# V loads asked for one window step earlier, first columns turned on GpSimd, and a different order at three joints of a fused attention, convolution and MLP kernel

## The chip, the cores and the metric

The kernel runs on one core of a Trainium2 chip. The metric is the device time of one execution in microseconds; the number given for a kernel is the median of its runs. Engines are called by their names: TensorE (PE, with its weight loads PEld), VectorE (DVE), ScalarE (ACT), GpSimd (POOL) and SyncE (SP), which issues the DMAs.

## The reference

The input x is 2 x 56 x 56 x 384 in float32. Two layers follow each other, everything in float32.

- Layer 0: `x = x + neighborhood_attention(layer_norm(x))`, with 12 heads of 32 channels. Each pixel attends to the 7 x 7 pixels around it (shifted inwards at the borders), with a relative position bias. Then `x = x + gelu(layer_norm(x) @ w1 + b1) @ w2 + b2`, 384 to 1536 and back.
- Layer 1: `p = layer_norm(x) @ w_in + b_in` (384 to 768 channels), a depthwise 3 x 3 convolution `local` of p, four exponential scans of it (`y = 0.6 * y_before + 0.4 * local`, along the rows in both directions and along the columns in both directions), `mixed = 0.25 * (their sum) + local`, then `x = x + layer_norm(mixed) @ w_out + b_out`, and again an MLP with gelu.

## The kernel before

The kernel writes out the order of each engine's instructions by hand; nothing is rescheduled behind it. An engine works through its list in order, and each instruction waits for what it reads and for the buffer that it writes.

**Attention.** The 2 x 56 x 56 pixels are 14 groups of 8 rows (448 pixels); each group is four windows of 8 x 14 queries, so 56 windows. A window has three units, one for four heads. The loop at L691 makes one step per unit, `s` from 0 to NU + 3 with NU = 168; `k = s % 12` is the step in the group and `hg = s % 3` the unit in the window. In step s, PE makes the scores of unit s (L508) into the two halves of a PSUM tile `sc`, then the values of unit s - 2 (L544 from `pts` and `vt`, and L550, the sums of the numerators through a matmul with ones). VectorE adds the bias to each half (L521), ScalarE takes the exponential (L528), VectorE adds up the numerators of unit s - 1 (L534, L536). After the last unit of a window the output is copied (`take`, L477), the sums are transposed and the 11 columns that are needed copied by GpSimd to `history` (`gather`, L481 and L482), inverted and spread (`invert`, L486 and L488), and multiplied in (`divide`, L492 and L494). Into most steps one more piece is put: queries, keys and values of later groups (L385, L423), or the projection of a finished tile (L569), whose result VectorE adds to the residual `xr` one step later (L577). In the last two groups (from `END` on) there is nothing left to compute ahead, and projections stand only in the steps of `THEN`.

`vt`, the values of a window's keys, comes back from `v_d` in DRAM in two or three DMAs when a `Window` is made (L464). SP's list in a step is, in order: stores of finished tiles (`store_all`, L629), loads of residuals (`load_residual`, L558), loads of later groups and biases (L301, L315), one of six parts of the MLP weights in the last steps (L612), and, where a window begins, its `vt`.

Before the loop, the first group is normalized and its queries, keys and values are made. Its four tiles are measured and applied in two halves (L632 to L643); group 1 and group 2 are normalized by ScalarE (`normalize_x`, L240), and turned by PE (`channels_of`, L356).

**Passes.** After the attention two passes go over groups of two to four tiles of 128 tokens. The first makes the MLP of layer 0 (12 chunks `hidden`, L1035 and L1044, then one `tokens` per tile, L1051, with the residual in L1381) and the projection `project_in` of the group before. The second (from L1413 on) makes the MLP of layer 1, with `measure` (transposes of `mix_d` by PE and statistics, L1238) of the next group beside its hidden chunks and `project_out` (L1258) after them.

**Beside.** Convolution and scans of layer 1 lie on VectorE beside the passes. `Beside` (L113) is a planner: `go(worth)` adds `worth` times a rate to a budget, and steps of the waiting jobs are issued until their costs have used it up; `until(name)` issues everything up to a named job. `Band` jobs make the convolution and the row scans of some rows, `Columns` jobs the column scans of one of 6 channel blocks of an image. A `Columns` job first turns half the image so that columns lie along the free axis (`turn`, four copies of 128 x 392, L1176, on ScalarE); the job behind another `Columns` is turned by the one before it, so that only the first of each image turns its own lines at its start. The second pass needs the second image's mixed values from group `half_way` on: at the end of group `half_way - 2` the planner runs `until((1, NI - 1))` and the group's `mx` is loaded (L1439, L1440).

## Time and profile before

| | |
|---|---|
| median of 3 runs | 2735.04 us (2734.52 to 2737.29) |
| the profiled execution | 2735.71 us, of which the span from first to last instruction is 2733.8 us |
| mean granted TensorE clock | 0.991 |
| DMA, mean over the span | 109 GB/s, 31% of the 16 engines' time |
| attention | up to about 708 us, its last projections to 722 us |
| first pass | from about 724 us to 1716 us |
| second pass | to the end; `mx` of the second image's first group is asked for at 2155 us |

A row of the timeline gives start, duration, engine, source line, operation, output and inputs, how many instructions are merged, and in brackets how long the engine was idle before it and what ended that. A line of the list of waits gives who waited for whom, the us in total, how often, and the longest. A row of a table of windows gives for each engine the busy us and the number of instructions, then the granted clock of TensorE (1.00 is full speed), the share of the DMA engines and GB/s. Many of PE's waits are shorter than 1 us; those that the change touches are shown in the prediction.

### The profile page before, as it was taken

How to read it: one execution, taken by the hardware profiler on the slowest of the kernel's cores; microseconds unless marked ns; L12 is line 12 of the kernel's file. 1: busy time of each engine (PE TensorE's matmuls, PEld its weight loads, DVE VectorE, ACT ScalarE, POOL GpSimd, SP SyncE). 2: the span in 40 equal slices, each digit the busy share in tenths (PEclk: the TensorE clock that was granted, in tenths of full speed). 3: DMA queues.
4: the chain of work that ended last, by engine and by line, in shares of the span. 5: the costliest groups of instructions: out<-in, count | busy, mean ns of one | idle time of the engine just before them, and what ended most of it. 6: DMA issues, size and time to landing. Idle time of an engine off the chain costs nothing. (4 is left out here: it accounts for less than half of the span.)

```text
span 2733.8 us, 36207 instructions
## 1 busy us (share of the span) xinstructions
PE 2686.1 (98%) x14975; PEld 1505.5 (55%) x14975; DVE 1663.0 (61%) x2449; ACT 907.5 (33%) x1455; POOL 239.1 (9%) x256
## 2 busy tenths in 40 slices
PE   8999999999899999999999999999999999999998
PEld 4566656665655555555545555455555555555565
DVE  3778767777421188688988889888798422221110
ACT  4555555554322332222344422311233211111111
POOL 0111111110211100000000000000000011110100
PEclk9999999999999999999999999999999999999999
DMA  6322444224411122232355444433454410011000
GB/s 206 131 93 92 155 165 150 76 74 154 155 35 38 63 88 103 86 129 101 120 184 195 180 151 154 163 128 114 147 200 158 151 47 25 28 44 35 29 12 16
DMA packets 131887, 298.91 MB, mean 109 GB/s; under 512 B 10646, under 2 KB 87552, under 8 KB 129408
## 3 DMA queue, kind: packets, MB, share of 16 engines
q1 hardware_dynamic: 131712, 296.50, 31.2%
q8 instruction: 119, 1.95, 0.3%
q14 instruction: 56, 0.46, 0.1%
HBM read 180.86 MB, written 115.61 MB: 108 GB/s over the span
## 5 line engine op out<-in xcount | busy, mean ns | idle before, releaser
L1035 PE MATMUL mm<-hT,w 128*128 128x512 f32 (+2 forms) x1872 | 778.7, 571 | 3.9 <-ACT hid L1044 3.8
L1051 PE MATMUL y<-w,hid 128*128 128x384 f32 x2352 | 764.8, 486 | 0.0
L1051 PEld LDWEIGHTS y<-w,hid 128*128 128x128 f32 x2352 | 445.0, 190 | 305.2 <-issue 0.5
L1035 PEld LDWEIGHTS mm<-hT,w 128*128 128x128 f32 x1872 | 352.5, 191 | 378.1 <-issue 343.1
L1044 ACT ACTIVATE hid<-mm,chan 128x512 f32<-128x512 f32 (+2 forms) x312 | 206.0, 661 | 744.8 <-PE mm L1035 744.7
L1129 DVE SCALAR_TENSOR_TENSOR loc<-pt,taps,loc 128x990 f32<-128x990 f32 (+9 forms) x336 | 377.0, 1122 | 8.3
L521 DVE TENSOR_TENSOR pts<-sc,bias 119x448 f32<-119x448 f32 (+3 forms) x336 | 220.8, 699 | 97.9 <-PE sc L508 97.0
L528 ACT ACTIVATE pts<-pts 119x448 f32<-119x448 f32 (+3 forms) x336 | 206.5, 641 | 194.6 <-DVE pts L521 194.4
L222 POOL TENSOR_TENSOR rs<-rs,mhalf 128x4 f32<-128x4 f32 (+4 forms) x67 | 87.3, 1303 | 1794.5 <-DVE rs L219 1788.0
L385 PE MATMUL ps<-hT,wqkv 128*128 128x448 f32 x504 | 211.5, 558 | 0.6 <-ACT hT L361 0.4
L1051 PE MATMUL y<-w_out,mx 128*128 128x384 f32 x588 | 193.7, 489 | 3.2 <-DVE xc L1258 3.2
L1035 PE MATMUL mm<-hT,w_in 128*128 128x512 f32 (+2 forms) x468 | 191.7, 568 | 0.6 <-ACT hT L254 0.6
L1381 DVE TENSOR_TENSOR xc<-y,xa 128x384 f32<-128x384 f32 x49 | 27.3, 557 | 252.1 <-PE y L1051 251.7
L1432 DVE TENSOR_TENSOR xc<-y,xc 128x384 f32<-128x384 f32 x49 | 27.2, 556 | 219.5 <-PE y L1051 169.2
L1051 PEld LDWEIGHTS y<-w_out,mx 128*128 128x128 f32 x588 | 112.5, 191 | 84.7 <-issue 6.8
L508 PEld LDWEIGHTS sc<-qT,kT 32*100 32x100 f32 (+3 forms) x3168 | 97.8, 171 | 91.3 <-DVE pts L521 17.7
L240 ACT ACTIVATE xn<-xc,sh,rs 128x384 f32<-128x384 f32 x98 | 64.7, 698 | 248.6 <-DVE sh L233 248.4
L1035 PEld LDWEIGHTS mm<-hT,w_in 128*128 128x128 f32 x468 | 88.8, 190 | 101.5 <-issue 91.6
L214 DVE BATCH_NORM_STATS2 st<-xi 128x6 f32<-128x384 f32 x98 | 50.3, 554 | 154.2 <-PE xi L1238 154.1
L508 PE MATMUL sc<-qT,kT 32*100 32x112 f32 (+3 forms) x3168 | 130.9, 279 | 8.6 <-DVE pts L521 7.8
L385 PEld LDWEIGHTS ps<-hT,wqkv 128*128 128x128 f32 x504 | 90.0, 191 | 79.5 <-issue 74.8
L254 ACT ACTIVATE hT<-tp,chan 128x512 f32<-128x512 f32 (+2 forms) x117 | 79.4, 750 | 152.5 <-PE tp L251 152.4
(88 smaller groups left out, 2421.5 us busy)
## 6 DMA issues: line engine op xcount, KB each, us to landing
bias<-in_bias_t SPq DMA_DIRECT2D x16, 1344.0 KB
loc<-loc_d SPq DMA_DIRECT2D x24, 784.0 KB
mixed<-mix_d SPq DMA_DIRECT2D x24, 784.0 KB
mix_d<-mixed SPq DMA_DIRECT2D x24, 784.0 KB
xa<-x_d SPq DMA_DIRECT2D x22, 768.0 KB
p_d<-mx SPq DMA_DIRECT2D x10, 1536.0 KB
mx<-mix_d SPq DMA_DIRECT2D x10, 1536.0 KB
pt<-p_d SPq DMA_DIRECT2D x18, 560.0 KB
```

Source lines behind the costliest of these rows:

```text
L214: nc.vector.bn_stats(st[:n, i, :], x)
L222: nc.gpsimd.tensor_tensor(rs, rs, mhalf[:n, :k], ALU.pow)
L240: nc.scalar.activation(out[:, k, :], x[:, k, :], AF.Identity, bias=self.sh[:n, k : k + 1], scale=self.rs[:n, k : k + 1],)
L254: nc.scalar.activation(dst[:, c, : len(xs) * n], tp, AF.Identity, bias=col(b, c), scale=col(g, c))
L385: nc.tensor.matmul(ps, lhsT=wqkv[:, c, m * P : (m + 1) * P], rhs=hT[:, c, half_of(n)], start=c == 0, stop=c == NC - 1,)
L508: nc.tensor.matmul(sc[i // 2][: w.keys, i % 2, c * TT : (c + 1) * TT], lhsT=kT[d, hg, w.keys_at + r * w.kc : w.keys_at + (r + w.rows) * w.kc],
L521: nc.vector.tensor_tensor(self.of(half), sc[half][:n, :, : self.m * TT].rearrange("p h (c q) -> p h c q", q=TT), self.w.bias[:n, 4 * self. ...
L528: nc.scalar.activation(self.of(half), self.of(half), AF.Exp)
L1035: nc.tensor.matmul(ps[:, : n * P], lhsT=w[:, c, m * P : (m + 1) * P], rhs=hT[:, c, : n * P], start=c == 0, stop=c == NC - 1,)
L1044: nc.scalar.activation(t[:, : n * P], ps[:, : n * P], AF.Gelu, bias=col(b1, m))
L1051: nc.tensor.matmul(ps, lhsT=t[:, k * P : (k + 1) * P], rhs=w[:, m, :], start=m == 0, stop=m == len(lhs) - 1,)
L1129: nc.vector.scalar_tensor_tensor(to, pt[:, lo + dy - self.top : hi + dy - self.top, xt : xt + n], self.tap(dy, dx), to, ALU.mult, ALU.add,)
```

## The change

The change has these parts.

- **V one step ahead.** A window, and with it the DMAs of its `vt`, is made in the last step (`hg == 2`) of the window before it instead of in its own first step; `vt` has three buffers instead of two. The first window is made ahead of the loop.
- **No history.** The sums of all windows are no longer kept: `gather` copies to a small tile `totals`, and `invert` multiplies two comparisons into a running tile `good` of 128 x 11. The two comparisons over 128 x 616 at the end are gone, and the reduction reads 11 columns. `turned` and `rec_t` share one buffer, and the operand of the value bias takes a buffer of `vs`.
- **First instructions.** Both halves of the first group are measured ahead of the first `apply`; group 2 is normalized by ScalarE ahead of the keys of group 1 instead of behind them.
- **First columns.** A `Columns` job that turns its own first lines does so with GpSimd's `tensor_copy`; the other turns stay on ScalarE.
- **A step dropped.** After the last tile of the last group of the first pass there is no `beside.go(ROW)`; ROW is 6.2.
- **Second image's first group.** For the group `half_way`, `measure` stands beside the hidden chunks 5, 7, 9 and 11 instead of 3, 5, 7 and 9, and its norm is closed at chunk 11 instead of 10.

```diff
--- before.py
+++ after.py
@@ -286,7 +286,8 @@
 
 
     BLOCKS = -(-NC * TT // HD)
-    history = lp.tile([P, len(windows), BLOCKS], F32, name="history")
+    good = lp.tile([P, BLOCKS], F32, name="good")
+    nc.vector.memset(good, 1.0)
     ones_hd = lp.tile([P, HD], F32, name="ones_hd")
     nc.vector.memset(ones_hd, 1.0)
 
@@ -433,7 +434,7 @@
 
     def shift_by_values(pool, psum, wproj, shift):
 
-        bv = pool.tile([P, NC, P], F32, name="bv")
+        bv = pool.tile([P, C], F32, name="vs", bufs=2).rearrange("p (c q) -> p c q", c=NC)
         for c in range(NC):
             nc.vector.tensor_copy(bv[:, c, :], col("b_v", c).to_broadcast([P, P]))
         ps = psum.tile([P, GT], F32, name="ps", tag="pt")[:, :C]
@@ -458,7 +459,7 @@
             self.keys = self.rows * self.kc
             self.keys_at = KEYS_AT[self.j]
             self.bias = biases[self.b, pr, pc]
-            self.vt = lp.tile([P, 3, C], F32, name="vt", bufs=2)
+            self.vt = lp.tile([P, 3, C], F32, name="vt", bufs=3)
             for c, a in enumerate(self.starts):
                 r = self.b * H + self.r0 + a
                 nc.sync.dma_start(
@@ -477,18 +478,23 @@
             nc.scalar.copy(self.og, o.rearrange("p c (r w) -> p c r w", r=QR))
 
         def gather(self):
-            turned = lp.tile([P, BLOCKS, HD], F32, name="turned")
+            turned = lp.tile([P, BLOCKS, HD], F32, name="turned", tag="turned")
             nc.vector.transpose(turned.rearrange("p a b -> p (a b)"), sums[:, : BLOCKS * HD])
-            nc.gpsimd.tensor_copy(history[:, self.i, :], turned[:, :, 0])
+            self.totals = sm.tile([P, BLOCKS], F32, name="totals")
+            nc.gpsimd.tensor_copy(self.totals, turned[:, :, 0])
 
         def invert(self):
             rec = sm.tile([P, BLOCKS], F32, name="rec")
-            nc.vector.reciprocal(rec, history[:, self.i, :])
+            nc.vector.reciprocal(rec, self.totals)
+
+
+            for edge, inside in ((SUM_MAX, ALU.is_le), (1.0 / SUM_MAX, ALU.is_ge)):
+                nc.vector.scalar_tensor_tensor(good, self.totals, edge, good, inside, ALU.mult)
             self.wide = lp.tile([P, BLOCKS, HD], F32, name="wide")
             nc.gpsimd.tensor_copy(self.wide, rec.unsqueeze(2).to_broadcast([P, BLOCKS, HD]))
 
         def divide(self):
-            rec = lp.tile([P, BLOCKS * HD], F32, name="rec_t")
+            rec = lp.tile([P, BLOCKS * HD], F32, name="rec_t", tag="turned")
             nc.vector.transpose(rec, self.wide.rearrange("p a b -> p (a b)"))
             rec = rec[:, : NC * TT].rearrange("p (c r w) -> p c r w", c=NC, r=QR)
             nc.vector.tensor_tensor(self.og, self.og, rec, ALU.mult)
@@ -630,15 +636,17 @@
 
 
     tps = [any_bank() for c in range(NC)]
-    for h in range(0, NT, 2):
-        norm = Norm(sm)
+    halves = [Norm(sm) for h in range(2)]
+    for h, norm in enumerate(halves):
         for k in range(2):
-            norm.add(k, [xgs[0][:, h + k, :]])
+            norm.add(k, [xgs[0][:, 2 * h + k, :]])
         norm.close(2, TT)
+    for h, norm in enumerate(halves):
         for k in range(2):
-            norm.apply(k, xgs[0][:, h + k, :], xgs[0][:, h + k, :])
+            x = xgs[0][:, 2 * h + k, :]
+            norm.apply(k, x, x)
             for c in range(NC):
-                turn_x(0, h + k, c, tps[c])
+                turn_x(0, 2 * h + k, c, tps[c])
     for c in range(NC):
         take_x(0, c, tps[c])
     nc.vector.tensor_scalar_mul(bq, chan[:, COL["b_qk"] : COL["b_qk"] + NC], HD ** -0.5)
@@ -663,11 +671,11 @@
     for t in tiles_of(1)[:2]:
         value(t, any_bank)()
         store_all()
+    for k in range(NT):
+        normalize_x(2, k)
     for m in range(NC, 2 * NC):
         query_or_key(1, m, any_bank)()
     store_all()
-    for k in range(NT):
-        normalize_x(2, k)
     for c in range(NC):
         channels_of(2, c, any_bank)()
     load_bias(0, 3)
@@ -685,6 +693,7 @@
 
     units, ws, to_project, ahead, taking = {}, {}, [], [], []
     ng = len(groups_a)
+    ws[0] = Window(0)
 
 
     END, THEN = ng - 2, (7, 9, 11, 13, 16, 19, 22)
@@ -718,6 +727,8 @@
             ectx.close()
             wm = ctx.enter_context(tc.tile_pool(name="w_mlp", bufs=1, side="right"))
             w1, w2, w_parts = weights(0)
+        if s < NU and hg == 2 and s + 1 < NU:
+            ws[i + 1] = Window(i + 1)
         if s >= NU - UG - 4 and hg == 2 and w_parts:
             w_parts.pop(0)()
         if s == NU:
@@ -737,8 +748,6 @@
             sctx.close()
             ps_s = sctx.enter_context(tc.tile_pool(name="a_pss", bufs=4, space=PSUM))
         if s < NU:
-            if hg == 0:
-                ws[i] = Window(i)
             units[s] = Unit(ws[i], hg)
             units[s].scores()
         new, before, last = units.get(s), units.get(s - 1), units.pop(s - 2, None)
@@ -799,12 +808,7 @@
         project(t, any_bank)()
     store_all()
 
-
     bad, flag = const.tile([P, 1], F32, name="bad"), const.tile([1, 1], mybir.dt.int32, name="flag")
-    every = history.rearrange("p w k -> p (w k)")
-    good = lp.tile(every.shape, F32, name="good")
-    nc.vector.tensor_scalar(good, every, SUM_MAX, 1.0, ALU.is_le, ALU.mult)
-    nc.vector.scalar_tensor_tensor(good, every, 1.0 / SUM_MAX, good, ALU.is_ge, ALU.mult)
     nc.vector.tensor_reduce(bad, good, axis=AX.X, op=ALU.min)
     nc.vector.tensor_scalar(bad, bad, -1.0, 1.0, ALU.mult, ALU.add)
     sctx.close()
@@ -1168,12 +1172,12 @@
                     for h in range(2):
                         nc.sync.dma_start(out=flat(self.loc[h]), in_=self.rows(loc_d, h))
 
-            def turn(self):
+            def turn(self, copy):
                 c, t = len(self.lines), half("line", "work")
                 for i in range(0, HALF, QUARTER):
                     for h in range(2):
                         at = slice(c * HALF + i, c * HALF + i + QUARTER)
-                        nc.scalar.copy(
+                        copy(
                             t[:, i : i + QUARTER, h * HALF : (h + 1) * HALF],
                             self.loc[h][:, :, at].rearrange("p h w -> p w h"),
                         )
@@ -1181,7 +1185,8 @@
 
             def steps(self):
                 if not self.lines:
-                    self.turn()
+
+                    self.turn(nc.gpsimd.tensor_copy)
                     yield 2.5
                 mixed, behind = [], None
                 for c in range(2):
@@ -1189,7 +1194,7 @@
                     for i in range(0, HALF, QUARTER):
                         yield from both_ways(t[:, i : i + QUARTER], t[:, i : i + QUARTER])
                         if c == 0 and i == 0:
-                            self.turn()
+                            self.turn(nc.scalar.copy)
                             for h in range(2):
                                 mixed.append(half("mixed", "out", 3))
                                 nc.sync.dma_start(out=flat(mixed[h]), in_=self.rows(mix_d, h))
@@ -1207,7 +1212,7 @@
                     if c == 0:
                         beside.behind()
                 if isinstance(behind, Columns):
-                    behind.turn()
+                    behind.turn(nc.scalar.copy)
                 for h in range(2):
                     def store(h=h):
                         nc.sync.dma_start(out=self.rows(mix_d, h), in_=flat(mixed[h]))
@@ -1241,12 +1246,13 @@
                 parts.append(ps.rearrange("p c q -> p (c q)"))
             norm.add(k, parts)
 
-        def measure_beside(m, g, ahead):
+        def measure_beside(m, g, ahead, late=0):
 
             n = dgroups[g][1]
-            if m % 2 == 1 and 0 < m // 2 <= n:
-                measure(ahead[0], ahead[2], m // 2 - 1)
-            if m == 10:
+            k = (m - late) // 2 - 1
+            if m % 2 == 1 and 0 <= k < n:
+                measure(ahead[0], ahead[2], k)
+            if m == min(10 + late, NHID - 1):
                 ahead[2].close(n)
 
         def project_out(g, mx, x, inner):
@@ -1380,7 +1386,8 @@
                 ps = tokens(hid, w2, k)
                 nc.vector.tensor_tensor(x2[:, k, :], ps, x[:, k, :], ALU.add)
                 norm.add(k, [x2[:, k, :]])
-                beside.go(ROW)
+                if g < last or k < n - 1:
+                    beside.go(ROW)
             norm.close(n)
             waiting = g, x2, norm
             if g + 2 <= last:
@@ -1415,7 +1422,7 @@
             for m in range(NHID):
                 hid.append(hidden(w1, m, hT, n, "L1_conv_b1"))
                 if g < last:
-                    measure_beside(m, g + 1, ahead)
+                    measure_beside(m, g + 1, ahead, 2 if g + 1 == half_way else 0)
                 beside.go(MLP_D)
             res = x3
             if g < last:
```

## Prediction

> **What bounds the kernel now.** I read the page's busy times first, then the list of PE's waits, then the stretches around each wait in the timeline and in tables of windows.
>
> ```profile
> PE 2686.1 (98%) x14975; PEld 1505.5 (55%) x14975; DVE 1663.0 (61%) x2449; ACT 907.5 (33%) x1455; POOL 239.1 (9%) x256
> ```
>
> TensorE is busy for 98% of the span, and the change leaves every matmul in place. So it can win only PE's 47.7 us of idle time and the time in which PE works at a lower clock. The waits of PE:
>
> ```profile
> PE ps L356 <- DVE xg L226: 7.8, 2, 6.0
> ...
> PE o L544 <- DMA vt<-v_d: 6.1, 4, 3.1
> PE mm L1035 <- ACT hid L1044: 3.8, 1, 3.8
> PE xi L1238 <- DMA mx<-mix_d: 3.5, 1, 3.5
> PE y L1051 <- DVE xc L1258: 3.2, 1, 3.2
> PE ps L356 <- ACT xg L240: 2.4, 4, 1.6
> ```
>
> Each part of the change has its row here: the first instructions (7.8 and 2.4), V (6.1), the first columns (3.8), the first group of the second image (3.5), and the step dropped at the end of the first pass (3.2). Columns: us in total, times, longest. The clock comes on top. In windows of 5 us in the last windows of the attention (busy us of PE, PEld, DVE, ACT, POOL; then the granted clock):
>
> ```profile
> 660.00:665.00 5.00, 5.00 (x26) 2.37 (x22) 0.60 (x2) 0.33 (x1) 0.00 (x0) 0.50 0.25 88
> ...
> 685.00:690.00 5.00, 2.53 (x40) 1.70 (x40) 1.38 (x3) 0.17 (x1) 0.00 (x0) 0.62 0.81 261
> ```
>
> At 660 PE is busy throughout at clock 0.50, and VectorE stands nearly still behind it: the projection L569 takes 4.21 us there and 2.20 at 668.59. So a stall costs its own length, and then some microseconds at half speed.
>
> **The rule on the clock, against the rows.** The Trainium skill, "TensorE: Matmul & The Clock Gate", section "What's actually happening", has the clock halve after an idle window of about 3.4 us. By that rule only the stalls of 3.81 and 3.47 us would drag a slow stretch behind them, and the clock would bring about 5 us less than below. The rows show more: half speed also follows the 3.23 us stall, and begins at 658.9, with PE merely thinned out (0.26 us busy in that microsecond). I follow the rows.
>
> **Opening (to 52 us).** Both halves of the first group are now measured before either is applied. VectorE's 1.6 us of statistics for tiles 2 and 3 (6.20 to 7.83) move into the wait for the power on GpSimd and ahead of the first applies. The second applies start at 7.07 (4.59 + 1.6 + 0.87) instead of 8.64, so 1.57 us earlier. PE's weight loads take 0.33 us instead of 0.19 until 13.99, and if that point stays put half is lost again: 0.8 to 1.57, I take 1.2. Moving ScalarE's four normalizations (2.49 us) ahead of the keys removes 1.59 + 3 x 0.28 = 2.43 us, as ScalarE is free from 37.6 and PE turns that tile only at 43.8. The key copies behind them come up to 0.8 us later; their banks are wanted again after 44, so nothing. The clock is 0.80 and 0.86 in the two windows after 45: (0.20 + 0.14) x 5 = 1.7 us. Sum 5.3, bounds 3 and 6. The bias operand now waits for a stored V tile's buffer; with its store out by 36 and PE reading at 46, that is covered.
>
> **V (590 to 708 us).** Before, vt was asked for in the step that starts the window, behind that step's store and residual load in SP's queue:
>
> ```profile
> 672.23 0.43 SPq L612 DMA_DIRECT2D w<-in_L_conv_w  x1
> 672.77 0.42 SPq L629 DMA_DIRECT2D x_d<-xr  x1
> 681.78 0.33 SPq L558 DMA_DIRECT2D xr<-in_x  x1
> 682.21 1.53 SPq L464 DMA_DIRECT2D vt<-v_d  x2
> ```
>
> The residual load waits for the store to land, which is behind the bias and 768 KB of weights, and vt behind it: 10 us late. Now the same loads stand one step earlier, and ahead of that step's weights: this one at about 672. A third buffer removes the wait for the values of the window before last. So all four vt waits go. In steps: the one at 656.7 gets back 1.24, then 2.01 in its projection and 0.45 in the next scores: 3.7. The one at 682.6 gets back 4.1, of which 0.5 is lost again to VectorE, whose 3.85 us of work in that step is next late: 3.6. The last gets 0.8. The slow projection at 678.44 (2.0) follows a wait for VectorE at 675.56, not for vt, so I count half: 1.0. Sum 9.1. SP now meets V's own stores sooner, in the step after they are issued; behind it stand only stores and loads for later steps.
>
> Against it stand 112 additions to VectorE, two updates of good per window. The nearest row is a 128x4 scalar_tensor_tensor at 0.16 us (bounds 0.07, a small memset, and 0.23, the 128x11 reciprocal): 0.32 per window. Up to 590 us VectorE waits for scores after them, 97 us in all, which covers them; uncovered they would cost 18. Of the ten windows after 590 I charge a third: 1.0. The two 128x616 checks at the end (0.47 + 0.80) were not on the path: PE restarts at 723.84, before they end. Net 8.1, bounds 3 (the stalls alone less 3.2) and 12.
>
> **First columns (1395 us).**
>
> ```profile
> 1394.55 0.92 ACT L1176 COPY line<-loc 128x392 f32<-128x392 f32 x1 [5.10 <-DMA loc<-loc_d]
> ...
> 1396.48 2.54 ACT L1176 COPY line<-loc 128x392 f32<-128x392 f32 x3 [1.02 <-DMA loc<-loc_d]
> ...
> 1400.26 11.06 PE L1035 MATMUL mm<-hT,w 128*128 128x512 f32 x18 [3.81 <-ACT hid L1044]
> ```
>
> ScalarE stands in front of these copies from 1389.45, three PSUM buffers fill, and PE stops. On GpSimd the copies block nobody: the next power in its queue comes 75 us later, in the second image 50 us. Gain 3.81, and weight loads 0.86 us apart instead of 0.43 until 1406.4, so 3.0 more: 6.8, bounds 3.5 and 7.5. In the second image ScalarE waits likewise at 1971, but no PE wait hangs on it: nothing. The price of a copy on GpSimd: nearest row wide, 352 elements in 0.48, so 0.53 each, 2.1 for four (ScalarE: 3.5). The rule that speaks against it is in "SBUF — State Buffer", "SBUF: two separate sides": GpSimd and a VectorE operation with two SBUF inputs lock each other out for a whole instruction. The rows agree that it bites: the power takes 1.01 alone and 1.75 to 2.4 beside VectorE's scans. At worst each copy waits out a scan of 1.79, 9.3 us for four. Only the scans of these lines wait for that, and no matmul, so the sum stays.
>
> **Dropped step (1716 us).**
>
> ```profile
> 1711.45 2.26 DVE L1076 TENSOR_TENSOR_SCAN both<-decay,loc 128x1008 f32<-128x1008 f32 x1
> ...
> 1715.31 0.62 DVE L1258 SCALAR_TENSOR_TENSOR xc<-y,rs,xa 128x384 f32<-128x384 f32 x1
> ...
> 1715.98 6.47 PE L1051 MATMUL y<-w_out,mx 128*128 128x384 f32 x14 [3.23 <-DVE xc L1258]
> ```
>
> Without the last go(ROW), taps and a scan (1706.33 to 1713.7) no longer stand before the norm's close and L1258. The wait of 3.23 goes, and 4.2 us at half clock behind it: 2.0. Sum 5.2, bounds 3 and 5.5.
>
> **Second image's first group (2165 us): here I expect no gain.** The dropped 6.2 credits are not given back. In the built order of VectorE, what is left after the last output add L1432 of the group before grows from the four updates at 2151.34 to four updates and three scans with their end fixes: 3.22 to about 8.7 us.
>
> ```profile
> 2150.86 0.56 DVE L1432 TENSOR_TENSOR xc<-y,xc 128x384 f32<-128x384 f32 x1 [1.94 <-PE y L1051]
> 2151.34 3.22 DVE L1202 SCALAR_TENSOR_TENSOR mixed<-line,mixed 128x392 f32<-128x392 f32 x4
> ...
> 2155.02 2.93 SPq L1224 DMA_DIRECT2D mx<-mix_d  x2
> ...
> 2164.59 1.51 PE L1238 MATMUL xi<-ident,mx 128*128 128x128 f32 x6 [3.47 <-DMA mx<-mix_d]
> ```
>
> The stores, and mx behind them, come 5.5 us later. Two chunks are 2 x 2.57 = 5.14 us. New wait: 3.47 + 5.5 - 5.14 = 3.8. Change: -0.4, bounds -4 and +5.6 (wait and slow clock both gone). Closing the norm at chunk 11 leaves about 2.7 us to the scale, under 3.9 us of matmuls and a second y buffer: nothing.
>
> **Sum.** 5.3 + 8.1 + 6.8 + 5.2 - 0.4 = 25.0. I take off 1.0 because the attention's last loads now come in less time and the wait at 723.84 (2.24, behind xa's landing) may grow. 24.0 from the span of 2733.8 gives 2709.8; the profiled execution was 2735.71 and gives 2711.7; the median of the runs, 2735.04, gives 2711.
>
> **Rivals.** (a) The two chunks do what they say: PE finds mx landed, 3.5 + 2.1 more: 2705. For it: two chunks exceed the old wait. Against it: the count of VectorE's leftover work. (b) The attention's end keeps its half clock: between scores PE still waits for VectorE at each step, as at 597 us without any vt wait. Then only the waits of 6.1 less 3.2 are won there: 2716. (c) Slower: the updates of good stand on the path. They have two SBUF inputs and are issued beside GpSimd's copy of wide (0.48). If each window's scores waited for 0.32 + 0.48 us, 56 windows would cost 45: 2735 - 25 + 45 = 2755. It decides from 0.45 us per window on. Against it: after the reciprocal VectorE often waits 1.2 to 2.6 us for scores.
>
> **Chances.** My forecast 0.56, own range 2706 to 2717; (a) 0.14; (b) 0.22; (c) 0.04; between no change and (b), several parts failing together, 0.04. From these: faster by over 0.2% (5.5 us, about what a measurement can tell from no change) 0.93, within 0.03, slower 0.04. The range 2702 to 2721 takes in (a), (b) and the bounds of the parts.
>
> **What would show it.** Right: no PE wait for vt, for hid at L1035 or for L1258; one for mx of about 4 us that stays; clock 1.00 after the former 1400 and 1716; first L385 matmul near 9.5; scores from about 46.5. Wrong: mx waits gone; clocks of 0.5 at the attention's end; the updates of good followed at once by L521 with PE waiting for it.

## The result and the profile after

The changed kernel takes 2716.53 us (median of 4 runs, 2715.67 to 2720.46), the kernel before beside it 2735.57 us: ratio 0.9931, 95% interval 0.9916 to 0.9947, so 19.0 us faster. The forecast was 2711 with a range of 2702 to 2721. A second comparison on another chip gave 2719.87 against 2734.78, ratio 0.9943 (0.9930 to 0.9957), 14.9 us. The forecast gain of 24 lies above both. The profiled execution took 2715.98 us with a span of 2714.2.

The busy times of the page, and the first rows of the list of PE's waits:

```profile
PE 2673.1 (98%) x14975; PEld 1500.2 (55%) x14975; DVE 1685.2 (62%) x2560; ACT 900.2 (33%) x1447; POOL 249.7 (9%) x264
```

```profile
PE sc L514 <- DVE pts L527: 8.2, 17, 1.1
PE ps L357 <- DVE xg L226: 7.0, 1, 7.0
PE tp L251 <- DVE bad L812: 6.6, 1, 6.6
PE xi L1243 <- DMA mx<-mix_d: 4.8, 1, 4.8
PE o L550 <- DMA vt<-v_d: 3.9, 6, 1.1
```

Gone are the waits for `hid` (3.8) and for `xc` of the output projection (3.2). The opening's 7.8 and 2.4 are one wait of 7.0. Two rows speak against the forecast: V is still waited for, six times, and the wait at the entry to the first pass (L251), 2.2 before, is 6.6.

The span fell by 19.6 us, PE's busy time by 13.0, its idle time by 6.6. With every matmul still there, less busy time is half clock that went, and stalls too short to be listed (the run with four times the updates shows such stalls). The windows of the attention's end that were shown for before:

```profile
660.00:665.00 5.00, 4.34 (x74) 2.74 (x74) 3.71 (x10) 1.56 (x4) 2.04 (x4) 1.00 0.60 192
...
685.00:690.00 5.00, 4.91 (x86) 3.08 (x82) 4.15 (x8) 2.43 (x5) 0.60 (x2) 1.00 0.31 91
```

Both stand at clock 1.00 (0.50 and 0.62 before). Only the second is a sign of the change: in the three kernels without V of the experiments below the window at 660 is at 1.00 too, and the one at 685 at 0.50 to 0.53.

**Where the time went, part by part.** The same VectorE instructions (transposes of the sums, additions of projections and of `tokens`) can be found in every profile; they are called marks here. How much earlier or later each comes than in the profile before tells what lies between two of them. I did this for the changed kernel and for all the kernels of the experiments below, since single profiles turned out to scatter. In the table, "with" are the profiles of kernels that hold the part, "without" those that do not (the one of before is 0 by definition); minus is earlier, in us.

| part, by the time of before | forecast | with | without | difference of means |
|---|---|---|---|---|
| opening, to 110 | -5.3 | -2.9 to -6.7 in nine profiles, mean -4.9 | 0, 1.1, -0.4, -0.5 | -4.9 |
| attention, 110 to 594 | 0 | 0.0 in each | 0 to 0.4 | 0 |
| V, 594 to the last unit at 708 | -8.1 | -6.8, -4.9, -6.5, -7.0, -6.9 | 0, 1.6, -0.5, -1.4 | -6.3 |
| 708 to the first pass's output at 751 | +1.0 | 5.2, 6.0, 6.1, 5.9, 0.8 | 0, -0.9, -0.5, -2.2 | +5.7 |
| first columns, 1376 to 1440 | -6.8 | -7.1 to -7.2 in ten profiles | 0, -0.5, -1.2, -0.5 | -6.6 |
| dropped step, 1705 to 1801 | -5.2 | -5.1 to -5.2 in ten profiles | 0, 0, -0.1, -1.7 | -4.8 |
| second image's group, 2151 to 2213 | +0.4 | 1.7, 1.1, 1.4, 2.4, 1.5, 1.5 | 0, 1.3, 1.0, -1.3 | +1.4 |

The differences add up to 15.5 us, between the two measured gains; the forecast's column to 24.0. V's two rows scatter most: from 594 to 751 together the five profiles with the part range from 1.1 later to 6.1 earlier, the four without from 0.6 later to 3.6 earlier. (Profiles of kernels that alter a part in a third way are left out of its row.)

### The profile page after: what moved, and what is told of

Read it like the earlier page. It is cut to its first block, busy times and chain, and to the rows that moved or that the text cites. A ratio compares the mean times of both kernels' runs of the same rounds, so it can differ in the third digit from the quotient of the medians.

```text
span 2714.2 us, 36305 instructions
## 1 busy us (share of the span) xinstructions
PE 2673.1 (98%) x14975; PEld 1500.2 (55%) x14975; DVE 1685.2 (62%) x2560; ACT 900.2 (33%) x1447; POOL 249.7 (9%) x264
## 5 line engine op out<-in xcount | busy, mean ns | idle before, releaser
L386 PE MATMUL ps<-hT,wqkv 128*128 128x448 f32 x504 | 211.9, 559 | 1.4 <-ACT vs L431 0.8
L1439 DVE TENSOR_TENSOR xc<-y,xc 128x384 f32<-128x384 f32 x49 | 27.2, 555 | 218.2 <-PE y L1055 167.8
L514 PEld LDWEIGHTS sc<-qT,kT 32*100 32x100 f32 (+3 forms) x3168 | 96.9, 169 | 91.2 <-DVE pts L527 18.5
L514 PE MATMUL sc<-qT,kT 32*100 32x112 f32 (+3 forms) x3168 | 130.1, 277 | 9.1 <-DVE pts L527 8.2
L386 PEld LDWEIGHTS ps<-hT,wqkv 128*128 128x128 f32 x504 | 90.2, 191 | 80.6 <-issue 74.8
```

Of the source, the lines that this page charges most:

```text
L386: nc.tensor.matmul(ps, lhsT=wqkv[:, c, m * P : (m + 1) * P], rhs=hT[:, c, half_of(n)], start=c == 0, stop=c == NC - 1,)
L514: nc.tensor.matmul(sc[i // 2][: w.keys, i % 2, c * TT : (c + 1) * TT], lhsT=kT[d, hg, w.keys_at + r * w.kc : w.keys_at + (r + w.rows) * w.kc],
```

## Experiments

The theory after the first profile: four of the forecast's terms hold; V's gain is given back before the first pass begins, through the landing of `xa` and GpSimd's queue; the dropped step's work comes back as a later `mx`. Rivals: the parts are not independent; the updates of `good` cost; DMA bandwidth and no queue is what makes things late; the list's own name for the wait at L251, the reduction `bad`.

### The four parts alone

Each is the kernel before with some hunks of the diff: the two hunks of the first instructions; those of V and of the history; those of `turn`; those of `measure_beside` and of the dropped `go`.

> The kernel before with the two reordered joints of the opening alone. Theory from the trace of the changed kernel: 6.4 us faster, 4.7 of it by 68 us and 1.7 more at 75 to 80 us, where the clock stays at 1.00 instead of 0.66; so about 2729. Rival, the forecast's term: 5.3, so 2730. A second rival: the 1.7 of clock is not owed to the reordering and comes and goes; then 4.7, 2730.5, and the trace shows the slow stretch at 75 to 80 us again.

Measured: 2729.89 us beside 2733.11, ratio 0.9984 (0.9978 to 0.9991). 4.5 us are won by 68 us and none at 75 to 80, where this profile has a slow stretch as before; the second rival describes it. That the stretch is not owed to the reordering is seen in the changed kernel itself. Windows of 5 us in the first profile of the changed kernel, then in its second:

```profile
70.00:75.00 5.00, 5.00 (x80) 3.20 (x75) 3.87 (x11) 2.54 (x7) 0.71 (x2) 1.00 0.37 121
75.00:80.00 5.00, 5.00 (x54) 3.11 (x53) 3.07 (x6) 2.66 (x6) 0.00 (x0) 1.00 0.44 127
```

```profile
70.00:75.00 5.00, 5.00 (x40) 3.33 (x41) 3.10 (x8) 2.03 (x5) 0.71 (x2) 0.50 0.31 102
75.00:80.00 5.00, 5.00 (x51) 2.74 (x50) 2.65 (x5) 1.53 (x3) 0.00 (x0) 0.84 0.12 42
```

The same code at the same place, once at 1.00 and once at 0.50 and 0.84: (0.50 + 0.16) x 5 = 3.3 us of difference that no line of the code makes, behind the same stall (PE is busy for 3.76 and 3.77 us between 65 and 70). The Trainium skill, "TensorE: Matmul & The Clock Gate", section "What's actually happening", says that the window in which activity is judged runs freely, and that the number of slow matmuls at a kernel's start therefore varies from run to run. These rows show such a variation in the middle of a kernel; that the free window is its cause is not shown. The runs of one kernel on one chip vary as well (the 21 of this one from 2724.9 to 2732.7). So a clock term that is read from one profile, as those of the forecast were, is a draw and not a constant.

> The kernel before with V asked for one step ahead, three vt buffers and the running good instead of the history, alone. Theory from the trace: the part wins 6.8 us net up to the last unit of the attention and gives 5.2 back before the first pass begins, because the inputs of the first pass (xa) and the last residuals come only 8.8 us earlier: net 1.6 us, 2733.5. Rival, the forecast: 8.1 less 1.0, so 7.1 us, 2728.5. Rival: the updates of good on VectorE cost more than they seem, net slower than 2735.6. Without the opening's gain DMA times are not moved relative to PE, so the waits for vt should look like those of the changed kernel: about six, 4 us together.

Measured: 2734.89 us beside 2733.11, ratio 1.0004 (0.9996 to 1.0013). V and the running `good` alone bring nothing that can be measured. The forecast's 7.1 is outside the interval (at best -1.1 us). In the profile 4.9 us are won between 594 and 708 and 6.0 given back by 751; the wait at L251 is 7.3. The theory's course is right, won and then given back; its net of 1.6 us faster is not, as it lies outside the interval too. The waits for `vt` were expected to be six with 4 us, and are four with 2.8. The last rival, a net loss, is not excluded: the interval reaches to 3.6 us slower.

> The kernel before with the first columns of each image turned by GpSimd, alone. Theory: one mechanism with one place, 7.2 us as the trace shows between 1390 and 1410, so 2728.4; the forecast's term 6.8, 2728.8. Rival: part of the 7.2 is owed to the earlier parts of the change (other distances on VectorE); then 3.8 to 6.

Measured: 2728.65 us, ratio 0.9984 (0.9977 to 0.9991), 4.5 us, which is the rival's number (3.8 to 6). But its reason is not seen: the profile has 7.1 between 1376 and 1440, the same as the profiles with all parts. Part of the difference is the draw of the clock in the profile before: where this part is not changed, the same stretch of other profiles is 0.5 to 1.2 shorter. That leaves 6.6, a little above the interval, which reaches to 6.3; the rest was not found.

> The kernel before with the dropped step at the end of the first pass and the later measurement of the second image's first group, alone. Theory from the trace: 5.2 won at 1716, 1.2 lost at 2165 where the wait for mx grows from 3.5 to 4.8 us: net 4.0, 2731.6. Rival, the forecast: 5.2 plus 0.4, 2730.0. Rival: the two chunks hide the wait in this setting, 5.2 plus 5.6, 2724.8. The four parts alone should add up to 19 if they are independent.

Measured: 2728.53 us, ratio 0.9987 (0.9978 to 0.9995), 4.6 us: the theory's 4.0 fits. (The expectation misquotes the forecast: its term for the second image's group was a loss of 0.4, so 4.8 for both, which fits as well.) In the profile -5.1 at 1716 and +1.7 at 2165. The wait for `mx` is 3.8 here; in kernels without this part it was 3.4 to 4.3.

### The changed kernel beside them

> The changed kernel itself, beside the kernel before on the chip of the other runs of this group. The four parts alone came to 3.2, -1.8, 4.5 and 4.6 us by the medians, 10.5 together. If the parts are independent, this kernel is about 10 to 12 us faster here, and the 19 us of the first comparison owed something to its chip or its few runs. Rival: the parts help each other, above all the opening and V at the attention's end, and it is again 17 to 20 us faster.

Measured: 2719.87 us, 14.9 faster than before (11.8 to 19.1 by the interval), between the two expectations. The four parts alone came to 10.5, each with 2 us of uncertainty. By the marks in their own stretches the single parts win 4.6 (opening), 7.1 (columns) and 3.5 (end) and lose 1.1 (V), 14.1 together, and this profile of the changed kernel wins 14.2. So there is no sign of parts that help each other much; but both comparisons of the whole (14.9 and 19.0) lie above 10.5, and whether a few us of it come from parts together stays open.

### The entry to the first pass

The end of the attention in the changed kernel. Rows of PE, SyncE's queue and GpSimd, by the timeline:

```profile
694.62 13.81 PE L575 MATMUL ps<-wproj,og 128*128 128x384 f32 x42
...
700.95 2.23 SPq L564 DMA_DIRECT2D xr<-in_x  x5
703.22 0.95 SPq L602 DMA_DIRECT2D xa<-x_d  x2
...
709.76 0.71 POOL L222 TENSOR_TENSOR rs<-rs,mhalf 128x2 f32<-128x2 f32 x1 [5.29 <-DMA xa<-x_d]
710.44 3.85 POOL L569 TENSOR_TENSOR xr<-xr,shift 128x384 f32<-128x384 f32 x4
...
715.02 1.51 PE L251 MATMUL tp<-ident,xn 128*128 128x128 f32 x6 [6.59 <-DVE bad L812]
```

PE's last projections end at 708.4. The additions of `shift` to the last four residuals stand in GpSimd's queue behind the norm's power, which waits for `xa`; the residual additions on VectorE wait for them, and PE, as it seems, for the PSUM of the projections: it begins 0.14 us behind the end of the last residual addition (714.88), as in the kernel before (0.15, from 723.69). From the start of the power to PE's first L251 it is 5.26 us here, 5.28 before (718.56 to 723.84) and 5.27 in the second profile (714.11 to 719.38): 0.68 of power, 3.85 of additions, 0.7 behind. In the run with the old chunks below, the projections ended 4 us later (712.4) and PE began at 715.00 all the same, 5.28 behind its power. So PE begins when `xa` lets it. `xa` is asked for behind a residual load that waits until a store has landed, and that store stands behind 768 KB of weights. (In the last windows of this profile the load that waits for such a store goes out 5.1 to 9.2 us behind it; behind the two stores with no weights right ahead of them, at 645 and 652, it is 2.5 and 3.7.) In the profile before this was so too, but PE came later and waited 2.2. V's gain of 13.2 at 708 (with the opening's) met an `xa` that landed only 8.8 earlier.

First edit: `xa` ahead of the residuals (the pools are opened with it), and the additions ahead of the norm.

```diff
         store_all()
+        if s == NU:
...
+            xs = {g: load_group(x1f, groups[g], "xa") for g in range(2)}
         while load:
             load_residual(load.pop(0))
...
         take()
+    for t in list(loaded):
+        add_bias(t)
     norm = norm_of(xs[0], groups[0][1], sm)
```

> The changed kernel, with the loads of xa ahead of the last residual loads in SyncE's queue and the additions of shift to the last residuals ahead of the norm's power in GpSimd's queue. Theory: the 5.2 us that were given back at the attention's end hang on the landing of xa (707.99) and on the power of its norm, which stands in GpSimd ahead of the four additions that the last projections wait for; then PE takes up the first pass at about 709 instead of 715.0, 6 us faster than the changed kernel, and the wait of 6.6 shrinks to about 1. Rival: the reduction named in the list of waits (bad, L812) is what PE waits for, or the landing of the last residual loads; then nothing, or under 2 us.

Measured: 2714.91 us beside 2719.87 of the changed kernel and 2734.78 of before, ratio to before 0.9928 (0.9915 to 0.9942): 5.0 better than the changed kernel by the medians, but not in the way expected. The wait at L251 shrank to 3.8 only, and PE began at 713.55. Now GpSimd's five additions waited for the residuals (they run from 705.88), the statistics of `xa` stood on VectorE behind the first residual addition until 707.38, and the power in GpSimd behind the five additions until 710.65. The second half of this edit, the additions ahead of the norm, had turned GpSimd's queue around for the worse.

Second edit, added to the first: `vt` straight behind `store_all()`, ahead of the residual.

```diff
         store_all()
...
+        if s < NU and hg == 2 and s + 1 < NU:
+            ws[i + 1] = Window(i + 1)
         while load:
             load_residual(load.pop(0))
...
-        if s < NU and hg == 2 and s + 1 < NU:
-            ws[i + 1] = Window(i + 1)
```

> The same, and a window's vt is asked for right behind the stores of its step, ahead of the load of the residual. Theory: the six waits for vt (3.9 us together) stay because vt stands in SyncE's queue behind a residual load that waits until a store has landed; they go, and since the attention's end no longer gives it back, the kernel is 10 us faster than the changed one (4 more than the one above). Rival: VectorE's work per step is next late, and PE waits for pts instead: 0 to 2 us more than the one above. Second rival: DMA bandwidth is what makes vt late; then the waits for vt stay.

Measured: 2712.72 us, ratio 0.9920 (0.9906 to 0.9934), 2.2 better than the one above, which the intervals do not tell apart. No wait for `vt` is left. But the edit moved less than it was meant to. A residual is loaded in the step of its store, and in the last windows that is mostly an earlier step than the one that asks for `vt`. So a single `vt` passes a residual load (it goes out at 652.86, the residual at 655.06), and the next three still stand behind one. SyncE in this run:

```profile
665.95 0.41 SPq L635 DMA_DIRECT2D x_d<-xr  x1
675.21 0.33 SPq L564 DMA_DIRECT2D xr<-in_x  x1
675.59 1.50 SPq L465 DMA_DIRECT2D vt<-v_d  x2
```

Those three go out 1.9 to 2.4 us earlier than in the run above. So the order of the queue has a part in it, but this run does not decide between queue and bandwidth; and three profiles with the old order have only 0.2 to 0.5 us of these waits. PE's waits for `pts` and `sum` of VectorE rose from 8.7 to 10.1, and the marks at 708 were 1.9 later than in the run above, as the rival has it. (In the next run, without this edit, they are 11.3.) The gain lies behind 708, where the residual load now goes out at 699.02 instead of 702.71.

Third: the first edit without the additions, GpSimd's queue left as it is.

> The changed kernel with the loads of xa ahead of the residual loads, and GpSimd's queue left as it is (power first, then the four additions). In the run that also turned GpSimd's queue around, the additions ran from 705.88 to 710.69 and the power only at 710.65, so PE began again at 713.55. Theory: with xa early and the power first, the power is done before the last residuals land, the four additions end near 711, and PE begins again at 711 to 712: 6 to 7 us faster than the changed kernel (5.0 by the medians with both edits). Rival: the power still waits for xa, since DMA traffic and not the queue's order delays it; then PE begins again at 714 or later, and it is within 3 us of the changed kernel.

Measured: 2712.97 us beside 2736.41, ratio 0.9917 (0.9904 to 0.9931), some 5.5 better than the changed kernel (whose ratios to before were 0.9931 and 0.9943). GpSimd and PE in this run:

```profile
707.07 0.71 POOL L222 TENSOR_TENSOR rs<-rs,mhalf 128x2 f32<-128x2 f32 x1 [2.28 <-DVE rs L219]
707.75 3.87 POOL L569 TENSOR_TENSOR xr<-xr,shift 128x384 f32<-128x384 f32 x4
...
713.05 0.84 PE L251 MATMUL tp<-ident,xn 128*128 128x128 f32 x6 [0.81 <-DVE bad L813]
```

The power waits for VectorE's own work and no longer for a transfer, PE waits 0.8, and the clock stays up (0.84 us for these six transposes instead of 1.51). The list still names `bad`, which follows the last residual addition at once; in the kernel before it came at 724.95, after PE had begun. So it was never what PE waited for. Between 594 and 751 this profile gains 7.9, the ones of the changed kernel 1.6 and 0.4. (The two runs below that leave this stretch as it is gain 1.1 and 6.1 there, so a single profile proves little; the four kernels with `xa` early gain 4.6 to 7.9.) PE begins 1 to 2 us later than I had expected, since its own projections ended at 712.2 here. So one order in SyncE's queue, and not V's own path, held most of what V should have brought: 4 to 7 us, by the runs' times and by the profiles.

### The second image's first group

```diff
-                beside.go(MLP_D)
+                beside.go(MLP_D + (ROW / NHID if g == 0 else 0.0))
```

> The changed kernel, and the 6.2 credits of the dropped step are given back in the second pass, 0.52 with each of the twelve hidden chunks of its first group. Theory: the wait for mx of 4.8 us at 2165 comes from work of the beside planner that the dropped step left over; VectorE's leftover after the last output addition falls from about 8.7 to 3.2 us, mx lands 5.5 us earlier and the wait goes: 5 to 7 us faster than the changed kernel. Rival: VectorE has no room in that first group, PE waits there for the statistics, and the gain is eaten: within 2 us. Second rival: the transfer of mx itself is slow, and 2 to 4 us of the wait stay.

Measured: 2711.98 us beside 2719.87 and 2734.78, ratio to before 0.9920 (0.9906 to 0.9933): 7.9 better than the changed kernel by the medians. VectorE ahead of the stores in the changed kernel, then in this one, from the output addition L1439 on:

```profile
2130.61 0.56 DVE L1439 TENSOR_TENSOR xc<-y,xc 128x384 f32<-128x384 f32 x1 [1.17 <-PE y L1055]
2131.09 1.78 DVE L1084 TENSOR_TENSOR_SCAN line<-decay,line 128x784 f32<-128x784 f32 x1
...
2136.51 3.20 DVE L1207 SCALAR_TENSOR_TENSOR mixed<-line,mixed 128x392 f32<-128x392 f32 x4
...
2150.82 1.51 PE L1243 MATMUL xi<-ident,mx 128*128 128x128 f32 x6 [4.80 <-DMA mx<-mix_d]
```

```profile
2130.78 0.56 DVE L1439 TENSOR_TENSOR xc<-y,xc 128x384 f32<-128x384 f32 x1 [1.94 <-PE y L1055]
2131.25 3.22 DVE L1207 SCALAR_TENSOR_TENSOR mixed<-line,mixed 128x392 f32<-128x392 f32 x4
...
2146.03 0.82 PE L1243 MATMUL xi<-ident,mx 128*128 128x128 f32 x6
```

The scans are no longer behind the last addition, and PE does not wait. Between 2151 and 2213 this profile gains 5.1, where the changed kernel loses 1.1 and 1.4: 6.4 us. In the first group, where the work went, nothing is lost (the marks from 1801 to 2126 stay at -20.1).

The other side, the old chunks with the dropped step:

```diff
-                    measure_beside(m, g + 1, ahead, 2 if g + 1 == half_way else 0)
+                    measure_beside(m, g + 1, ahead)
```

> The changed kernel with the second image's first group measured beside chunks 3, 5, 7 and 9 again, the dropped step left out as in the changed kernel. The forecast's sum for the wait for mx was 3.47 + 5.5 - 5.14. By it the wait is 4.8 + 5.1 = 9.9 us here and the kernel 5 us slower than the changed one. Rival: the matmuls of the two chunks move behind the wait but the clock is at half speed behind the longer wait, 7 us or more. Second rival: mx lands no later for the dropped step, the later chunks were not needed; then the wait is near 4 and the time the same.

Measured: 2723.33 us beside 2736.41, ratio 0.9957 (0.9943 to 0.9971). Row of the waits:

```profile
PE xi L1243 <- DMA mx<-mix_d: 9.9, 1, 9.9
```

9.9 is the sum 4.8 + 5.1 to the tenth, so two chunks are worth what the forecast took for them. The ratio is 5.5 us above the mean of the changed kernel's two. The stretch from 2151 to 2213 is 6.4 us longer than in the mean of its two profiles, so some 1.3 of it would be half clock behind the longer wait (the window of 5 us in which the wait ends and the next one are at 0.50 and 0.57, in the changed kernel at 0.66 and 1.00). The later chunks only pay for the dropped step.

### The updates of good

```diff
-            for edge, inside in ((SUM_MAX, ALU.is_le), (1.0 / SUM_MAX, ALU.is_ge)):
+            for edge, inside in 4 * ((SUM_MAX, ALU.is_le), (1.0 / SUM_MAX, ALU.is_ge)):
```

> The changed kernel with the two updates of good issued four times over in each window: 0.96 us more of VectorE in each of 56 windows, the same result. Theory: up to about 594 us PE does not wait for them, and only the last ten windows, where VectorE is next late, pay part of it: 3 to 8 us slower than the changed kernel, and the marks of the windows up to 594 us stay where they are. Rival, the forecast's slower case: scores wait for VectorE from 0.45 us per window on; then 0.96 us each, up to 54 us slower, and the loss grows from window to window from the start.

Measured: 2747.71 us, ratio to before 1.0043 (1.0029 to 1.0057), about 29 us slower than the changed kernel by the ratios. The expectation fell, and with it the 0.96 us. The updates of 43 windows, the third to the 45th, in the changed kernel and then in this one (busy us of VectorE at L492, and the number of updates):

```profile
83.00:594.00 511.00, 20.97 (x86) 1.00 0.36 117
```

```profile
83.00:613.00 530.00, 88.41 (x344) 1.00 0.35 117
```

So 67 us were added in these windows, 1.57 in each, and 16 in the last eleven (19.10 against 3.04). Most updates take 0.10 to 0.17 us. But 22 of the changed kernel's 112 take 0.38 to 0.92, and 97 of the 448 here 0.33 to 0.95; each of these ends, to within 0.04 us, with an instruction that GpSimd runs beside it, an addition of `shift` or the copy of `wide`. Two of them in the changed kernel, 0.80 and 0.38 long, between their neighbours on GpSimd:

```profile
467.80 0.99 POOL L569 TENSOR_TENSOR xr<-xr,shift 128x384 f32<-128x384 f32 x1
468.01 1.22 DVE L492 SCALAR_TENSOR_TENSOR good<-totals,good 128x11 f32<-128x11 f32 x2
468.73 0.48 POOL L494 COPY wide<-rec 128x352 f32<-128x352 f32 x1
```

In the changed kernel the copy of `wide`, which the forecast's rival (c) had named, holds up ten updates, and the addition, which nobody had counted, twelve. Up to 594 us the marks fall behind by 13.8 (from +5.6 at 83 to +19.4), a fifth of what was added there, and in the last eleven windows by 23.6, half as much again as was added. The list of waits does not show the first: between 80 and 590 us PE waits 2.0 for `pts` in the changed kernel, and 2.5 in the same work here. It is in the busy time. A window of the changed kernel and one of this kernel with as many matmuls, 6864:

```profile
80.00:590.00 510.00, 507.64 (x6864) 309.57 (x6862) 402.85 (x823) 278.05 (x504) 73.84 (x131) 1.00 0.37 120
```

```profile
80.00:605.00 525.00, 520.97 (x6864) 317.37 (x6862) 459.58 (x1074) 277.01 (x507) 72.56 (x129) 1.00 0.36 118
```

13.3 us more of "busy" PE for as many matmuls at the same clock of 1.00. Taken one by one, the 6732 matmuls between 85 and 585 us of the changed kernel last 499.9 us there and 513.6 here, and 13.1 of the 13.7 us lie at the scores (L514): the waits are there, most of them cut into pieces that count as work. For the two updates that the change makes, the marks say what the list could not: from 110 to 594 us the changed kernels keep their distance to before within 0.1 us, so there they cost nothing, though they keep VectorE busy for 26.0 us in all and not for the forecast's 18.

### All in one kernel

The changed kernel with `vt` and `xa` ahead of the residual and the credit given back.

> All that the runs point to in one kernel: the changed kernel, vt asked for ahead of the residual, xa ahead of the residual, and the 6.2 credits given back in the first group of the second pass. Theory: the three places are independent; by the medians of the runs before, 7.2 for the first two and 7.9 for the third, so 15 us faster than the changed kernel and about 30 us faster than the kernel before, ratio 0.989. Rival: at the attention's end VectorE and the clock at half speed take back what vt gives; then 12 to 13 us faster than the changed kernel.

Measured: 2708.13 us (2707.36 to 2711.72) beside 2736.41, ratio 0.9902 (0.9887 to 0.9918): 27 us faster than the kernel before by the ratio, the fastest of all, and 10 faster than the changed kernel (0.9902 against 0.9937, the mean of its two). The theory's 15 is not reached. By the marks it is 13 against the changed kernel, the rival's number: between 594 and 751 this profile gains 7.4 (1.6 and 0.4 there), from 2151 to 2213 it gains 5.1 (1.1 and 1.4 lost there). The 7.4 are no more than the 7.9 of `xa` alone, so the one `vt` that passes a residual load adds nothing that these profiles show once `xa` is early.

## Why the prediction was right, and where it was not

- **The time.** 2716.5 lies in the range and 5.5 above the forecast; by the second comparison's ratio it would be 2720, in the range by 1 us. Of the 8.5 us between the forecast's 24.0 and the table's 15.5, 4.7 are what V gave back, 1.8 V's own size, 1.0 the second image's group, and the other three parts 1.0 together. For two of these, columns and dropped step, the profile before had drawn its stretches of half clock a little long (others without the part are up to 1.2 and 1.7 shorter there).
- **Opening, 5.3.** Right: 4.9. Scores begin 4.0 to 5.5 earlier. The first L385 matmul (L386 now) starts at 9.94 instead of near 9.5, since both halves of the group are now turned in one piece after a wait of 7.0.
- **V, 8.1.** "So all four vt waits go" was wrong in the first profile: of 6.1 us, 3.9 were left, and again in the second. The loads stand one step earlier but behind the same kind of residual load. SyncE in the changed kernel:

```profile
668.60 0.41 SPq L635 DMA_DIRECT2D x_d<-xr  x1
677.77 0.33 SPq L564 DMA_DIRECT2D xr<-in_x  x1
678.15 1.51 SPq L465 DMA_DIRECT2D vt<-v_d  x2
```

  Nine microseconds between the store and the load that waits for it, as before; I had put `vt` in the right step and not looked at what is ahead of it in that step. The load goes out at 678.15 and not at about 672. In the other profiles with the same `vt` order 2.8, 1.8, 0.5, 0.3, 0.2 and 0 us of the waits were left, and where it was 0.2 to 0.5 the waits for `pts` were 9.6 instead of 8.0 to 8.2. Nor was 6.1 a constant of the kernel before: in the three kernels without V these waits are 10.5 to 11.8. The size of the term up to the last unit, 6.3, is near; since the loads did not go out as early as its working has it, that is in part luck.
- **"I take off 1.0 because the attention's last loads now come in less time".** The step that failed, by its size: the mechanism and the place are right, it is 5.7. The profile before had the number. From the landing of `xa` to PE's start it was a fixed chain, and PE had only 2.2 us of wait ahead of it; whatever V wins beyond what `xa` wins is lost one for one. I should have followed `xa` to its issue (710.68) and to the store that it queues behind, and asked by how much that moves.
- **Updates of good, 1.0 in the last ten windows.** Up to 594 they cost nothing, as said. After it they were not measured alone and are within V's net. "97 us in all, which covers them" was the wrong reason: with 67 us added, less than the 97, 14 were paid. (The 97 is VectorE's wait for scores at L521 in the whole attention, and not only behind the place of the updates.) VectorE's idle time is not free in the windows in which PE's scores follow closely. And the price of an update, 0.16 us from the nearest row, left out what GpSimd does beside it: it is 0.23 us in the mean and up to 0.92.
- **First columns, 6.8.** Right: 6.6. The copies took 0.91 us (median of eight) and not 0.53, up to 2.4 beside VectorE, and it did not matter, since no matmul waits for them. ScalarE's queue is free, as GpSimd's rows show, which now hold the copies:

```profile
1387.54 0.90 POOL L1180 COPY line<-loc 128x392 f32<-128x392 f32 x1
1388.70 4.13 POOL L1180 COPY line<-loc 128x392 f32<-128x392 f32 x3 [0.26 <-DMA loc<-loc_d]
```

- **Dropped step, 5.2.** Right: 4.8, and 5.2 against the profile before. PE runs through its 48 matmuls with `w_out` (1689.68 to 1705.32) without a wait.

- **Second image's group, a loss of 0.4.** No gain, as said against rival (a), and the reason is shown by the run that gave the credit back. The wait is 4.8 and not 3.8, the net a loss of 1.4. VectorE's leftover has the forecast size: from the last output addition to the stores it is 8.35 us (2130.61 to 2138.96), 2.94 before, 5.4 more. What was 1.1 off is the transfer: from the stores to PE's start 11.9 us instead of 10.8. Why it takes longer was not found.
- **Rivals.** (a) fell. (b), 2716, named the nearest time, but for another reason: the half clock at 685 did go (that at 660 is missing without V too), and the gain was lost behind 708. (c) was not in the measurement. The run with four times the updates shows its mechanism in part: scores do wait for the updates, but up to 594 us for a fifth of their time.

## What to carry to other kernels

When a change makes a stage shorter, follow the first load of the next stage back to what it queues behind: a chain from a landing transfer to the first matmul does not shrink with the stage, and the list of waits names the last link of it and not the first. Work that the planner no longer did at one place came back at another, and giving it a place of one's choice (12 small portions where PE did not mind) was worth as much as the whole saving. And a term of one or two microseconds that is half clock cannot be read from one profile: compare the same instruction's time across several, with and without the part.

## What the runs showed of the hardware that was not expected

- The same instructions at 70 to 80 us ran at clock 1.00 in one profile of the changed kernel and at 0.50 and 0.84 in another; runs of the kernel before on one chip spread from 2728.3 to 2738.5.
- PE's busy time for windows of 6864 matmuls at clock 1.00 was 507.6 us in one kernel and 521.0 in another, with 2.0 and 2.5 us of listed waits: short stalls between small matmuls are counted as busy (13.1 of the 13.7 us that the same matmuls took longer lay at the scores).
- A stall of 2.24 us ahead of L251 was followed by half clock (1.51 us for six transposes), one of 2.63 (in the run with the old chunks) was not (0.85), nor one of 2.91 (first columns alone, 0.84).
- A 128x11 update on VectorE took 0.10 to 0.17 us in 90 of 112 cases of the changed kernel and 0.38 to 0.92 in the other 22, each of which ended with a copy (0.48) or an addition (0.99) that ran beside it on GpSimd.
